# Graph layer on one core: output sums by DMA between DRAM tensors, earlier constants and loads, another general path

## The chip, the cores and the metric

One Trainium2 chip; the kernel runs on one of its cores, in one launch. The metric is the device time of an execution in microseconds (us). All times in this document are in us unless another unit stands beside them.

## The reference

x has N = 1250 nodes with D = 1024 features, in float32. There are E = 20000 edges (src, dst) with a type out of R = 8, and dst is sorted.

```python
h = jnp.maximum(_layernorm(x, axis=-1), 0.0)
# relational graph convolution on h, with edge_index = (src, dst)
u = h @ root + bias
for r in range(8):
    mask = edge_type == r
    sums = segment_sum(h[src] * mask[:, None], dst, N)
    cnt = segment_sum(mask, dst, N)
    u = u + (sums / maximum(cnt, 1)[:, None]) @ weight[r]
# highway
z = concatenate([u, h], axis=1) @ w_gate + b_gate
out = x + tanh(u) * z + h * (1 - z)
```

root and each weight[r] are 1024 x 1024, w_gate is 2048 x 1024.

## The kernel before, in words

**Order of the mathematics.** The kernel multiplies first and gathers afterwards: y = h @ weight[r] is computed for all nodes and stored to DRAM, and for each destination the rows y[src] of its edges are gathered and summed with their factors (1 / count). The output is made as (x + h) + the highway's rest: x + h is stored to `out` early, and at the end blocks of rows are scattered onto `out` by DMAs that add.

**Products.** Eleven matrices s are multiplied with the 1250 rows: s = 0 to 7 the relations, 8 the root, 9 (`LAST`) the lower half of w_gate, which meets h, and at the end the upper half, which meets u. The product is Strassen-Winograd's: seven smaller products, the *kinds* n = 0 to 6, of sums of quarters of h (left) with sums of quarters of the matrix (right), and each kind is again split in seven, with *inner sums* made beside it. s = 0 is done by blocks of rows (`product`, matmuls on L576), since the rows come in while it runs; s = 1 to 9 by kinds (`kind`). In a kind, in this order: two plain products into `xs`, then `left_sum(0)` x `right(0)` into the bank `ps_q`, `left_sum(1)` x `right(1)`, a plain one, DVE's additions on L427, `left_sum(2)` x `right(2)` into the bank that L427 has just read, and so on. TensorE's matmuls all have the lines L321 and L328.

**Inner sums.** `inner_sums(m, n, second)` makes them half by half. The right ones come from DVE (L276, L277 and L282, L283). The left ones are the same for every matrix: DVE makes them for s = 1 (L285, L286 and L279, L280), they are stored to `lefts_dram`, and for s > 1 a DMA on SP's queue loads each half (512 KB, L274), from the place in program order where the half's right sums are made. `loaded(s, n)` says for which kinds; with `LOADED = {}` for all but (9, 5) and (9, 6).

**What stands beside the products.** The program is written in one order, and each engine follows that order for its own instructions; SP's DMA queue too. The other work is spread over it by Python generators: within a kind, `call(k)`, k = 0 to 4, advances the generator by one `yield`. For the first two and a half matrices that generator is `norms_and_index` (L1346). Its parts:

- `norms()`: in s = 0 loads blocks of x, makes h = relu(layernorm(x)) in `Normed`, stores h to `h_dram`, and calls `with_x` (L1005): DVE adds x and h (L1009), SP stores the sum to `out` (L1010). The blocks are brought into the transposed layout `h_all` by DMA transposes (L540) with copies by ACT (L547) and DVE (L558).
- `columns()`: sorts out for every destination a table of its edges. Its last step is a DMA from POOL, table <- bits (L1213). Then the pool of buffers that it used is closed.
- `order()`: opens the pool "sort" in that room, and puts the nodes of each of three groups of relations in the order of their number of edges. `positions` (L864) begins with three iotas and a memset on POOL (L868 to L871), then compares on DVE (L872 to L874, L879, L885, ...) and makes ranks; `nodes_in_order` does one group's permutation with matmuls, and issues ten index gathers on POOL, idx <- table (L715). At the end `any_over` checks for destinations with too many edges.

The calls (4, k) for all k and (n, 3) for all n (`FULL_CALLS`, L78) are passed over. When `norms_and_index` has ended, the calls advance `beside_group`: for each of the three groups `counts(g)`, which counts edges by relation on DVE (memset L1384, pairs L758 and L759 over the index table).

At kind (3, 0) (L1690 to L1696) whatever is left of `beside_group` is flushed, and then `counts_over` (L1657) writes a branch that all engines pass: `If n_far > 0` (L1664) holds the general path for edges that fit no table (`far_ranks`, `order_again`, `counts`, `passes_over`). With this data it is not entered. From (3, 1) on the gathers begin: POOL's indirect DMA got <- y, idx (L1405), and DVE's multiply-add (L1410), for one slot of a block of 128 destinations.

**The end.** The last matrix is multiplied by blocks again, and `scatter_outs` adds finished blocks of rows to `out` (L726). The last block, of 98 rows, is scattered in pieces of columns, `PIECES`: one of 512 columns, then two of 256.

Of the kernel before, what the change touches and what calls it, by code (L numbers as in the profile page):

```python
# [9 lines left out]
F32 = mybir.dt.float32  # L10
BF16 = mybir.dt.bfloat16
# [10 lines left out]
def tile_rgcn_highway(  # L22
# [58 lines left out]
    LOADED = {}  # L81
# [45 lines left out]
    z_dram = dram.tile([N, D], F32, name="z_dram")  # L127
    codes_dram = dram.tile([WIN + NCH * P], I16, name="codes_dram")
# [134 lines left out]
    def inner_sums(m, n, second):  # L263


        b11, b12, b21, b22 = quarters(m.factor(n))
        a11, a12, a21, a22 = [left_of(n, o, k) for o in (0, 1) for k in (0, 2)]
        t1, t2, t3, t4 = [right(k) for k in range(4)]
        s1, s2, s3, s4 = [lefts[:, k].rearrange("p (u f) -> p u f", u=2) for k in range(4)]
        both = slice(2 * second, 2 * second + 2)  # L270
        kept = lefts_dram[n].rearrange("p (k n) -> p k n", k=KQ)[:, both]
        from_dram = loaded(m.s, n)
        if from_dram:
            nc.sync.dma_start(lefts[:, both], kept)  # L274
        if second:
            nc.vector.tensor_sub(t3, b22, b12)  # L276
            nc.vector.tensor_sub(t4, b21, t2)  # L277
            if not from_dram:
                nc.vector.tensor_sub(s3, a11, a21)  # L279
                nc.vector.tensor_sub(s4, a12, s2)  # L280
        else:
            nc.vector.tensor_sub(t1, b12, b11)  # L282
            nc.vector.tensor_sub(t2, b22, t1)  # L283
            if not from_dram:
                nc.vector.tensor_add(s1, a21, a22)  # L285
# [10 lines left out]
    def kind(m, n, between):  # L296
# [92 lines left out]
        if chained:  # L389
            rest()  # L390
            alone(range(KQ))
            alone_rows()
            call(0)
            m.make(n)
            for j, i in enumerate((0, 2, 1, 3)):
                add(banks[i], h_op[i][:, ORDER[n]], w, fresh=n not in (1, 5))
                if i == 2:
                    to_rows_of(0)
                if i == 0:
                    next_sums()  # L400
                call(j + 1)
            to_rows_of(1)
            return
# [22 lines left out]
        for u in range(2):  # L426
            nc.vector.tensor_add(banks[2 * u][:, H:], xs[u], ys[:, u * H:(u + 1) * H])  # L427
        call(1)
# [11 lines left out]
        for u in range(2):  # L440
            add(banks[2 * u][:, H:], left_sum(3)[:, u], b22)
        to_rows_of(0)
# [323 lines left out]
    def nodes_in_order(g, pos, ids_f, a, b, small, now=False, fresh=True):  # L766
# [5 lines left out]
        many = small[:, :P].bitcast(I16)[:, :P]  # L772
        hi_i, lo, hi, block = [small[:, P + k * ND:P + (k + 1) * ND] for k in range(4)]
        hi_i, lo, hi = hi_i.bitcast(I32), lo.bitcast(I16)[:, :ND], hi.bitcast(I16)[:, :ND]
        if fresh:
            nc.gpsimd.iota(many, pattern=[[1, P]], base=0, channel_multiplier=0)
            nc.vector.tensor_copy(block, many[:, :ND])
# [12 lines left out]
        while not now and at_call[2] != 2:  # L790
            yield
# [53 lines left out]
    def positions(runs, pos, ids_f, room, now=False):  # L845
# [17 lines left out]
        runs3 = runs.rearrange("p (g d) -> p g d", g=G)  # L863
        picked = room[1][:, :NHI * NCNT]  # L864
# [3 lines left out]
        nc.gpsimd.iota(many, pattern=[[1, P]], base=0, channel_multiplier=0)  # L868
        nc.gpsimd.iota(n_of, pattern=[[-1, NCNT]], base=SLOTS, channel_multiplier=0)
        nc.gpsimd.iota(step_of, pattern=[[1, ND], [-1, ND]], base=0, channel_multiplier=0)  # L870
        nc.gpsimd.memset(ones, 1.0)  # L871
# [26 lines left out]
        while not now and at_call[2] != 2:  # L898
            yield
# [23 lines left out]

    def passes_over():

        top = const.tile([1, 1], F32, name="top")
        largest((most[:, 0:1], top))
        whole(top, n_over, MORE - SLOTS, 0.0)
        nc.vector.tensor_single_scalar(n_over, n_over, 2, op=OP.arith_shift_right)
# [10 lines left out]
    with ExitStack() as early:  # L940
# [20 lines left out]
        class Normed:  # L961
# [43 lines left out]

            def with_x(self, to=None):
                n = self.n
                to = self.xt if to is None else to
                nc.vector.tensor_add(to[:n], self.xt[:n], self.ht[:n])  # L1009
                nc.sync.dma_start(out[self.d * P:self.d * P + n, :], to[:n])  # L1010
# [76 lines left out]
        runs = ix1.tile([P, NHI], F32, name="runs")  # L1087

# [127 lines left out]
        def order():  # L1216

            checks = [any_over]

            def rest_of_check():  # L1220
                if checks and at_call[0] and at_call[2] == 2:
                    checks.pop()()

            with tc.tile_pool(name="sort", bufs=1) as sp:
                pos = sp.tile([P, NHI], F32, name="pos")
                yield from positions(runs, pos, ids_f, [
                    sp.tile([P, n], F32, name=f"counted{k}")
                    for k, n in enumerate((D, *(NHI * NCNT // (1, 2, 2)[k] for k in range(3))))])
# [27 lines left out]
        def norms():  # L1256
# [12 lines left out]
            for b in b0:  # L1269
                b.with_x()  # L1270
# [4 lines left out]
            for b in b1:  # L1275
                b.with_x()
# [9 lines left out]
            b2[0].with_x(b2[0].ht)  # L1286
            b2[1].with_x()
# [19 lines left out]
            for b in b3:  # L1307
                b.with_x()
# [10 lines left out]
            for part in range(2):  # L1319
                ht = xpool.tile([P, D], F32, name="xt") if part else \  # L1320
                    h_op[4][:, S3:S4 + 1].rearrange("p a k f -> p (a k f)")
                if part:
                    b4[0].with_x()
# [10 lines left out]
            b4[1].with_x()  # L1334
# [10 lines left out]

        def norms_and_index():  # L1346

            later = index()
# [4 lines left out]
            for _ in later:  # L1353
                yield
# [18 lines left out]
    with ExitStack() as edges_part:  # L1373
# [264 lines left out]
        def order_again():  # L1638

            t = got()  # L1640
            runs, pos, ids_f = t[:, :NHI], t[:, NHI:2 * NHI], t[:, 2 * NHI:2 * NHI + ND]
            nc.vector.tensor_copy(ids_f, ids)
            in_table, is_edge = [
# [5 lines left out]
            room = [upool.tile([P, D], F32, name="u") for _ in range(4)]  # L1649
            for _ in positions(runs, pos, ids_f, room, True):  # L1650
                pass
            for g in range(G):
                for _ in nodes_in_order(g, pos[:, g * ND:(g + 1) * ND], ids_f,
                                        got().bitcast(BF16), got().bitcast(BF16), got(), True):
                    pass
# [115 lines left out]
        PIECES = ((2, Q), (4, H), (4, 0))  # L1771
# [96 lines left out]
        for i in range(NP):  # L1868
# [85 lines left out]
```

## Time and profile before

| | us |
|---|---|
| three timed runs | 1287.15, 1291.23, 1292.73 (median 1291.23) |
| the profiled execution, its own time | 1288.27 |
| its span, from first to last instruction | 1286.5 |
| PE busy | 1252.6 |
| DVE busy | 973.6 |
| POOL busy | 435.0 |
| ACT busy | 274.0 |

The granted clock of TensorE was 0.992 over the span. The DMA queues moved 315.90 MB, 246 GB/s on the mean.

PE is TensorE's matmuls, DVE the vector engine, ACT the scalar engine, POOL GpSimd; SPq is the queue of instructions of the sync engine, which here issues most DMAs. A row of a timeline gives the start, the duration, the engine, the line, the operation with what it writes and reads (buffer numbers left out), the shape and how many instructions are put together in the row; the bracket is the idle time of the engine just before, and what ended it ("issue": nothing that the profile shows). A row of a group gives the count, the busy sum and the mean in ns, then the idle time before. A row of the DMA issues gives the count and the KB of each or the median time from issue to landing. `out_dram<-h_all` or `<-xt` is the store of x + h, `counted` and `small` are buffers of the pool "sort", `bits` and `raw` of the pool before it.

### The profile page before, as it was taken

What the parts mean: (1) busy time and instruction counts of PE and PEld (TensorE: products, weight loads), DVE (VectorE), ACT (ScalarE), POOL (GpSimd) and SP (SyncE); (2) the same over time, 40 slices, a digit from 0 to 9 for tenths busy, and PEclk for the clock granted to TensorE, in tenths of its full rate; (3) what the DMA queues carried; (4) which work ended last, traced back from release to release, by engine and by line L of the source; (5) the groups of instructions that cost most, each with busy time, mean ns of one, the idle gap of its engine ahead of it and who ended that gap; (6) DMA issues with size and microseconds to landing.
All of it is one profiled execution on the core that took longest, in us unless ns stands there. A gap on an engine that the chain in (4) does not pass through costs nothing.

```text
span 1286.5 us, 14084 instructions
## 1 busy us (share of the span) xinstructions
PE 1252.6 (97%) x4725; PEld 885.3 (69%) x4725; DVE 973.6 (76%) x1459; ACT 274.0 (21%) x517; POOL 435.0 (34%) x393
## 2 busy tenths in 40 slices
PE   9999999899999999999999999999999999999996
PEld 5444777677767777777777777777777777544443
DVE  7665998676758787887887779898888797856642
ACT  3353211121112112112111211211221121202210
POOL 0430000017102222322432333463452467754532
PEclk9999999899999999999999999999999999999999
DMA  7786324834656686998898768899997969999983
GB/s 301 239 239 195 126 90 169 205 108 137 194 175 206 202 276 236 314 319 317 293 331 302 248 192 289 286 334 352 352 288 250 357 190 356 349 335 225 234 151 56
DMA packets 131088, 315.90 MB, mean 246 GB/s; under 512 B 30963, under 2 KB 32382, under 8 KB 131006
## 3 DMA queue, kind: packets, MB, share of 16 engines
q1 hardware_dynamic: 87678, 189.79, 42.6%
q0 software_dynamic: 43040, 124.60, 32.7%
q8 instruction: 38, 0.62, 0.2%
q10 hardware_dynamic: 288, 0.52, 0.1%
q14 instruction: 44, 0.36, 0.1%
HBM read 251.70 MB, written 85.06 MB: 262 GB/s over the span
## 4 chain that ended last, share of the span: by engine, by line
PE 45%; issue 9%; DMA 8%; POOL 6%; DVE 2%; ACT 0%; POOLq 0%; SPq 0%; DVEq 0%; ACTq 0%
PE ps_n L321 15%; PE ps L321 14%; PE ps_b L328 10%; DMA got<-y,idx 7%; PE ps_q L321 5%; POOL got L1405 2%; POOL out_dram L726 1%; PE ps_b L576 1%; POOL h_all L715 1%; DMA w<-lefts_dram 1%; POOL u L715 1%; PE ps_n L576 1%; DMA z_dram<-w 0%; DVE u L1410 0%; POOL w L715 0%
## 5 line engine op out<-in xcount | busy, mean ns | idle before, releaser
L1405 POOL DMA_INDIRECT got<-y,idx x205 | 253.3, 1236 | 446.8 <-DVE u L1410 338.7
L321 PE MATMUL ps<-w,h_all 128*128 128x256 f32 (+1 forms) x1040 | 258.7, 392 | 0.0
L1410 DVE SCALAR_TENSOR_TENSOR u<-got,w_of,u 128x1024 f32<-128x1024 f32 (+1 forms) x189 | 241.1, 1277 | 16.2 <-DMA got<-y,idx 15.8
L321 PE MATMUL ps_n<-w,w 128*128 128x256 f32 x976 | 236.3, 386 | 10.8 <-DVE ps L427 6.9
L321 PEld LDWEIGHTS ps_n<-w,w 128*128 128x128 f32 x976 | 187.3, 193 | 64.1 <-issue 23.8
L328 PE MATMUL ps_b<-w,h_all 128*128 128x512 f32 x504 | 226.6, 592 | 0.0
L321 PEld LDWEIGHTS ps<-w,h_all 128*128 128x128 f32 x1040 | 197.6, 190 | 39.7 <-issue 14.1
L328 PEld LDWEIGHTS ps_b<-w,h_all 128*128 128x128 f32 x504 | 95.8, 190 | 94.1 <-issue 90.9
L576 PE MATMUL ps_b<-w,h_all 128*128 128x512 f32 x312 | 140.0, 594 | 4.5 <-ACT h_all L547 1.6
L321 PE MATMUL ps_q<-w,w 128*128 128x256 f32 x488 | 116.1, 381 | 4.3 <-DMA w<-lefts_dram 2.2
L436 ACT COPY ps<-ps_n 128x512 f32<-128x512 f32 x122 | 64.6, 574 | 255.7 <-PE ps_n L321 255.7
L321 PE MATMUL ps<-w,w 128*128 128x256 f32 x488 | 116.3, 381 | 0.0
L321 PE MATMUL ps_n<-w,h_all 128*128 128x256 f32 x488 | 115.3, 379 | 0.4 <-PEq L1664 0.4
L576 PEld LDWEIGHTS ps_b<-w,h_all 128*128 128x128 f32 x312 | 58.3, 190 | 78.5 <-issue 68.6
L427 DVE TENSOR_TENSOR ps<-ps_n,inner 128x256 f32<-128x256 f32 x122 | 50.4, 429 | 75.7 <-PE ps L321 75.6
L321 PEld LDWEIGHTS ps_q<-w,w 128*128 128x128 f32 x488 | 92.6, 190 | 18.1 <-issue 2.5
L321 PEld LDWEIGHTS ps<-w,w 128*128 128x128 f32 x488 | 93.6, 192 | 13.0
L321 PEld LDWEIGHTS ps_n<-w,h_all 128*128 128x128 f32 x488 | 92.6, 190 | 13.8 <-PEq L1664 0.8
L413 ACT COPY ps<-ps_n 128x256 f32<-128x256 f32 x122 | 39.6, 360 | 245.6 <-PE ps_n L321 184.1
L236 DVE TENSOR_TENSOR w<-w,w 128x2048 f32<-128x2048 f32 x36 | 82.2, 2284 | 0.3
L576 PE MATMUL ps<-w,h_all 128*128 128x512 f32 (+1 forms) x136 | 57.7, 568 | 1.4 <-DVE h_all L558 1.4
L1213 POOL DMA_DIRECT2D table<-bits x1 | 1.7, 1707 | 145.5 <-DVE bits L1212 145.5
(250 smaller groups left out, 1181.4 us busy)
## 6 DMA issues: line engine op xcount, KB each, us to landing
w<-lefts_dram SPq DMA_DIRECT2D x108, 512.0 KB
w<-in_L_gnn_weight_dram SPq DMA_DIRECT2D x31, 1024.0 KB
y<-row SPq DMA_DIRECT2D x84, 256.0 KB
y<-w SPq DMA_DIRECT2D x42, 256.0 KB
w<-in_L_gnn_w_gate_dram SPq DMA_DIRECT2D x8, 1024.0 KB
lefts_dram<-w SPq DMA_DIRECT2D x14, 512.0 KB
h_dram<-h_all SPq DMA_DIRECT2D x9, 512.0 KB
y<-row SPq DMA_DIRECT2D x9, 512.0 KB
```

Source lines behind the costliest of these rows:

```text
L236: nc.vector.tensor_sub(w[to], w[a], w[b])
L321: nc.tensor.matmul(p, a[:, k], b[:, k], start=(fresh and k == 0), stop=(k == a.shape[1] - 1), skip_group_check=True)
L328: nc.tensor.matmul(to, h_op[NP - 1][:, ORDER[n], k], w[:, k], start=(fresh and k == 0), stop=(k == KQ - 1), skip_group_check=True)
L413: nc.scalar.copy(banks[2 * u][:, :H], xs[u])
L427: nc.vector.tensor_add(banks[2 * u][:, H:], xs[u], ys[:, u * H:(u + 1) * H])
L436: nc.scalar.copy(banks[2 * u + 1].rearrange("p (a n) -> p a n", a=2), xs[u][:, None, :].to_broadcast([P, 2, H]))
L576: nc.tensor.matmul(b[:, at], aop[:, i, k, :], w.of[i][:, k, at], start=(fresh and k == 0), stop=(k == KQ - 1), skip_group_check=True)
L715: nc.gpsimd.indirect_dma_start(out=to, out_offset=None, in_=of, in_offset=bass.IndirectOffsetOnAxis(ap=at, axis=0), compute_op=op)
L726: ins = nc.gpsimd.indirect_dma_start(out=of, out_offset=bass.IndirectOffsetOnAxis(ap=at, axis=0), in_=frm, in_offset=None, compute_op=op)
L1213: nc.gpsimd.dma_start(table.rearrange("(b p s) o -> p b (s o)", p=P, s=SLOTS), rows_in)
L1405: nc.gpsimd.indirect_dma_start(out=t[:n], out_offset=None, in_=y[g][:, :], in_offset=bass.IndirectOffsetOnAxis(ap=at[:n, d, k:k + 1], axis=0),
L1410: nc.vector.scalar_tensor_tensor(u[:n], t[:n], w, u[:n], op0=OP.mult, op1=OP.add)
```

## The change

1. **x + h.** `with_x` and its ten calls are removed. SP copies x to `out` from DRAM to DRAM, two blocks of 128 rows at a time, at call 1 of kinds n = 0, 1, 2, 3 and 5 of s = 1. In `order`, after each group's nodes, POOL issues DMAs that add h from `h_dram` onto `out`, also from DRAM to DRAM, 3, 3 and 4 of them. After the groups come two additional yields.
2. **Constants of `order`.** `positions` is started early: its iotas and the memset run at the start, into a buffer `counted0` of an older pool (`ix1`), as does `pos`. The first comparisons (L872 to L874) also use only that pool; L879 is the first to use "sort". `nodes_in_order` takes the iota `many` from there.
3. **Loads of left sums.** `load_sums` issues the load of a kind's first half before `call(1)` of the kind before, and of the second half after `left_sum(3)` of the kind before. `LOADED` leaves out (8, 5), (9, 1) and (9, 3): DVE makes these sums.
4. **General path.** `order_again` ranks nodes by comparing counts with a broadcast from DRAM, without TensorE, and `passes_over` transposes by DMA.
5. **Pieces.** The last block's scatter is two pieces of 512 columns.

```diff
-    LOADED = {}
+    LOADED = {8: (0, 1, 2, 3, 4, 6), 9: (0, 2, 4)}
...
-        if from_dram:
-            nc.sync.dma_start(lefts[:, both], kept)
...
+    def load_sums(s, n, second):
+
+        if n == 7:
+            s, n = s + 1, 0
+        if s <= LAST and loaded(s, n) and not regular(s, n):
+            both = slice(2 * second, 2 * second + 2)
+            nc.sync.dma_start(lefts[:, both],
+                              lefts_dram[n].rearrange("p (k n) -> p k n", k=KQ)[:, both])
...
             nc.vector.tensor_add(banks[2 * u][:, H:], xs[u], ys[:, u * H:(u + 1) * H])
+        load_sums(s, n + 1, 0)
         call(1)
...
             add(banks[2 * u][:, H:], left_sum(3)[:, u], b22)
+        load_sums(s, n + 1, 1)
         to_rows_of(0)
...
+        nc.gpsimd.iota(many, pattern=[[1, P]], base=0, channel_multiplier=0)
+        nc.gpsimd.iota(n_of, pattern=[[-1, NCNT]], base=SLOTS, channel_multiplier=0)
+        nc.gpsimd.iota(step_of, pattern=[[1, ND], [-1, ND]], base=0, channel_multiplier=0)
+        nc.gpsimd.memset(ones, 1.0)
+        yield many
         picked = room[1][:, :NHI * NCNT]
...
-            def with_x(self, to=None):
-                n = self.n
-                to = self.xt if to is None else to
-                nc.vector.tensor_add(to[:n], self.xt[:n], self.ht[:n])
-                nc.sync.dma_start(out[self.d * P:self.d * P + n, :], to[:n])
...
+        pos = ix1.tile([P, NHI], F32, name="pos")
+        counted = [ix1.tile([P, D], F32, name="counted0")]
+        placing = positions(runs, pos, ids_f, counted)
+        many = next(placing)
...
+                counted.extend([sp.tile([P, NHI * NCNT // n], F32, name=f"counted{k}")
+                                for k, n in ((1, 1), (2, 2), (3, 2))])
+                yield from placing
...
                 for g in range(G):
-                    yield from nodes_in_order(g, pos[:, g * ND:(g + 1) * ND], ids_f, junk, hot, room,
-                                              fresh=g == 0)
+                    yield from nodes_in_order(g, pos[:, g * ND:(g + 1) * ND], ids_f, junk, hot, room, many)
+                    assert not xh
+                    for d in range(g * ND // G, (g + 1) * ND // G):
+                        nc.gpsimd.dma_start(out[block(d)], h_dram[block(d)], accum_op=OP.add,
+                                            max_dma_last_dim=4 * D)
+                for _ in range(2):
+                    yield
                 while checks:
...
+            for d in range(ND):
+                xh.append((out[block(d)], x[block(d)]))
             later = index()
...
             for _ in later:
+                if xh and at_call[0] == 1 and at_call[2] == 1:
+                    for _ in range(2):
+                        nc.sync.dma_start(*xh.pop())
                 yield
...
+            for g in range(G):
+                for half in range(2):
+                    at = slice(half * KEYS // 2, (half + 1) * KEYS // 2)
+                    nc.gpsimd.dma_start(v_bc, val_dram[g:g + 1, at].to_broadcast([P, KEYS // 2]))
+                    for c in range(g * ND, (g + 1) * ND):
+                        to = pos[:, c:c + 1]
+                        nc.vector.scalar_tensor_tensor(junk, v_bc, val[:, c:c + 1],
+                                                       one.to_broadcast([P, KEYS // 2]),
+                                                       op0=OP.is_gt, op1=OP.mult,
+                                                       accum_out=part if half else to)
+                        if half:
+                            nc.vector.tensor_add(to, to, part)
...
-        PIECES = ((2, Q), (4, H), (4, 0))
+        PIECES = ((2, Q), (2, 0))
...
-                if more is not None:
+                if more is not None and c0 == 0:
                     scatter_piece(c0, t[1])
```

More of the change, by code (lines that the diff above doesn't have):

```diff
@@ L789, in nodes_in_order @@
         yield
-        while not now and at_call[2] != 2:
+        while at_call[2] != 2:
             yield
@@ L843, in to_table, with positions @@
         rests()
-    def positions(runs, pos, ids_f, room, now=False):
+    def positions(runs, pos, ids_f, room):
         used = [0]
@@ L897, in positions @@
         yield
-        while not now and at_call[2] != 2:
+        while at_call[2] != 2:
             yield
@@ L1268, in norms @@
             yield
-            for b in b0:
-                b.with_x()
             yield
@@ L1638, in order_again @@
         def order_again():
+            sizes = (NHI, NHI, NHI, NHI, ND, 1, 1)
             t = got()
-            runs, pos, ids_f = t[:, :NHI], t[:, NHI:2 * NHI], t[:, 2 * NHI:2 * NHI + ND]
+            runs, val, pos, pos_i, ids_f, one, part = [
+                t[:, sum(sizes[:k]):sum(sizes[:k + 1])] for k in range(len(sizes))]
+            pos_i = pos_i.bitcast(I32)
             nc.vector.tensor_copy(ids_f, ids)
+            nc.vector.memset(one, 1.0)
             in_table, is_edge = [
```

65 lines of the change are left out of this document (32 added, 33 removed).

## The prediction

> **What bounds the kernel now.** The page first: its span and its line of engines.
> ```profile
> span 1286.5 us, 14084 instructions
> PE 1252.6 (97%) x4725; PEld 885.3 (69%) x4725; DVE 973.6 (76%) x1459; ACT 274.0 (21%) x517; POOL 435.0 (34%) x393
> ```
> PE is busy for 97%. An edit that takes work from DVE, POOL or a queue therefore pays only where PE waits. The timeline of PE is read next, for gaps (the bracket is the idle time before the row's first matmul, and what ended it).
> ```profile
> 60.87 3.70 PE L576 MATMUL ps_b<-w,h_all 128*128 128x512 f32 x8 [0.93 <-ACT h_all L547]
> 65.93 3.70 PE L576 MATMUL ps<-w,h_all 128*128 128x512 f32 x8 [1.36 <-DVE h_all L558]
> 87.43 3.70 PE L576 MATMUL ps_b<-w,h_all 128*128 128x512 f32 x8 [0.63 <-ACT h_all L547]
> ...
> 247.53 3.78 PE L321 MATMUL ps_n<-w,w 128*128 128x256 f32 x8 [6.13 <-DVE ps L427]
> 251.10 2.87 PE L321 MATMUL ps<-w,w 128*128 128x256 f32 x8
> 257.26 1.89 PE L321 MATMUL ps_q<-w,w 128*128 128x256 f32 x8
> ...
> 367.18 1.97 PE L321 MATMUL ps_n<-w,h_all 128*128 128x256 f32 x8 [0.45 <-PEq L1664]
> 371.28 2.53 PE L321 MATMUL ps_q<-w,w 128*128 128x256 f32 x8 [2.13 <-issue]
> 373.61 3.05 PE L321 MATMUL ps_n<-w,w 128*128 128x256 f32 x8
> ...
> 918.42 1.97 PE L321 MATMUL ps_q<-w,w 128*128 128x256 f32 x8 [1.44 <-DMA w<-lefts_dram]
> 1028.70 1.97 PE L321 MATMUL ps_q<-w,w 128*128 128x256 f32 x8 [0.76 <-DMA w<-lefts_dram]
> 1096.06 3.68 PE L321 MATMUL ps_n<-w,w 128*128 128x256 f32 x8 [3.31 <-ACT ps L413]
> ```
> Eight undisturbed matmuls of this shape take 1.97. After a gap they are slower: 3.78 and 2.87 behind 6.13 idle, together 6.65 - 2 x 1.97 = 2.7 more; 3.68 behind 3.31 idle, 1.7 more. I call this the ramp and add it to a gap. Each part of the change aims at one of these gaps.
>
> **Part 1, x + h to the output.** In the first matrix SP stores x + h, made by DVE, and its queue is in order.
> ```profile
> 46.88 0.98 SPq L1010 DMA_DIRECT2D out_dram<-h_all  x2
> 48.86 7.57 SPq L540 DMA_TRANSPOSE inner<-h_all  x1
> ...
> 59.48 1.33 ACT L547 COPY h_all<-inner 128x1024 uint16<-128x1024 uint16 x1 [5.79 <-DMA inner<-h_all]
> ```
> The transpose is issued behind two 512 KB stores; the ACT copy waits 5.79 for it, and PE's gap at 60.87 waits for that copy. The two other gaps of the first matrix have the same chain behind them. Without the stores I take all three as gone: 0.93 + 1.36 + 0.63 = 2.9 (bounds: nothing, and 3.6 with slower matmuls behind them). The ten DRAM copies move to the second matrix, two at a time over five calls on SP.
> ```profile
> DMA  7786324834656686998898768899997969999983
> ```
> A digit is a slice of 32.2; that matrix lies in the slices from 129 to 257, with 3, 2, 4 and 8 tenths. There is room, so I cost the copies at nothing (at most 1, if a load behind them is late). The ten accumulating DMAs on POOL are a rival below.
>
> **Part 2, order's constants.** POOL's and DVE's timelines around 247:
> ```profile
> 233.05 1.71 POOL L1213 DMA_DIRECT2D table<-bits  x1 [145.49 <-DVE bits L1212]
> 245.97 0.23 POOL L868 IOTA counted<- 128x128 int16 x1 [11.22 <-DMA table<-bits]
> ```
> ```profile
> 247.38 0.90 DVE L879 TENSOR_TENSOR counted<-runs,counted 128x720 bf16<-128x720 f32 x1
> 252.16 0.68 DVE L282 TENSOR_TENSOR w<-w 128x512 f32<-128x512 f32 x1
> ```
> L868 writes into a pool that opens where another closes, whose last user, the table's DMA, lands at 245.97. DVE's comparisons wait for the iota, L427 is queued behind them, and PE for L427: 6.13 + 2.7 = 8.8. After the change iotas and first comparisons lie in an older pool: L427 no longer waits and PE starts at 247.53 - 6.13 = 241.4. But L879 is the first touch of the reopened pool, and I expect it to wait for the same DMA. It then begins at 245.97 instead of 247.38, 1.41 earlier, and L282, queued behind it, ends at 252.84 - 1.41 = 251.4. PE's work from 247.53 to ps_q takes 257.26 - 247.53 - 2.7 = 7.0, so PE comes to ps_q at 248.4 and waits 3.0 for L282; with 1.7 of ramp ps_q is as far along at 253.1 as before at 257.26: 4.1 gained. Bounds: 8.8 gained if L879 doesn't wait; 1 lost if the table lands later. I take 4.1, since L868 waited though its bytes need not be those that the DMA reads.
>
> The Trainium skill ("TensorE: Matmul & The Clock Gate", Part 1) has the array at half clock only after an idle window of about 3.4 us. By it the new gap of 3.0 has no ramp and the sum would be 1.7 lower. The trace disagrees: 2.53 and 3.05 stand behind an idle of 2.13.
>
> **Part 3, the general path and two more yields.** At 367 all engines pass the branch L1664 around the general path. PE's gaps 0.45 + 2.13 and the slower matmuls (2.53 + 3.05 - 3.94 = 1.6) are 4.2 in all; a body with under half of PE's instructions should take them away. But DVE passes too:
> ```profile
> 366.33 0.94 DVE L448 TENSOR_TENSOR ps<-ps,inner 128x256 f32<-128x256 f32 x2 [0.60 <-PE ps L321]
> 373.73 1.29 DVE L379 TENSOR_TENSOR w<-w,ps 128x512 f32<-128x512 f32 x2 [6.46 <-issue]
> ...
> 378.42 0.43 DVE L427 TENSOR_TENSOR ps<-ps_n,inner 128x256 f32<-128x256 f32 x1 [0.36 <-PE ps L321]
> ```
> ```profile
> 381.82 1.73 PE ps_n L321 x8
> ```
> DVE loses 6.46 here. The two yields put the check of order two calls later, so that the generator of the counts has one call left before the branch, where the rest is flushed: counts(1) and counts(2).
> ```profile
> L1384 DVE MEMSET got<- 128x1024 f32 x3 | 2.7, 912 | 0.5 <-issue 0.5
> L758 DVE TENSOR_SCALAR got<-idx 128x220 f32<-128x220 int32 x8 | 2.2, 270 | 0.8 <-issue 0.5 <-DMA idx<-table,node_key 0.3
> L759 DVE TENSOR_REDUCE got<-got 128x10 f32<-128x220 f32 x8 | 3.1, 384 | 0.3
> ```
> Two groups are two memsets and five pairs: 2 x 0.91 + 5 x (0.27 + 0.38) = 5.1, with their share of the idle and small sums about 6.1. DVE ends L448 at 367.27; with 6.1 and 6.46 L379 starts at 379.8. From L379 to the end of the second L427 DVE has 4.1 of work (378.85 - 373.73, less waits of about 1): 383.9. The matmuls that need it began at 381.82: 2.1 late. PE, no longer stalled itself, would be there at 381.82 - 4.2 = 377.6, idles over 6 us and pays a ramp of 2.7: 4.8 lost. Bounds: 3.9 gained (no flush in the way: DVE at 377.9), 4.8 lost. I take the loss.
>
> **Part 4, left sums.** SP's timeline, the loads behind the gaps at 918 and 1028:
> ```profile
> 904.94 0.32 SPq L274 DMA_DIRECT2D w<-lefts_dram  x1
> ...
> 1018.09 0.38 SPq L274 DMA_DIRECT2D w<-lefts_dram  x1
> ```
> SP runs ahead of the engines and issues a load when the buffer is free, unless a store stands before it. The first was issued 13.5 before its use; an earlier place can't help, the transfer itself was slow: nothing. The second came late behind stores: 0.8 gained. Three kinds, (8,5), (9,1), (9,3), are no longer loaded; 6 of 108 loads go and DVE makes those sums with four additions each, of about 0.68:
> ```profile
> L285 DVE TENSOR_TENSOR w<-h_all 128x512 f32<-128x512 f32 x7 | 4.8, 684 | 0.0
> ```
> ```profile
> 1083.95 1.89 PE L321 MATMUL ps_n<-w,w 128*128 128x256 f32 x8
> ```
> ```profile
> 1053.11 0.69 DVE L337 TENSOR_TENSOR row<-row,ps_b 128x512 f32<-128x512 f32 x1 [1.50 <-PE ps_b L328]
> ...
> 1082.03 0.76 DVE L427 TENSOR_TENSOR ps<-ps_n,inner 128x256 f32<-128x256 f32 x2
> 1088.58 1.28 DVE L1410 SCALAR_TENSOR_TENSOR u<-got,w_of,u 128x1024 f32<-128x1024 f32 x1 [4.61 <-DMA got<-y,idx]
> ```
> That is 2.7 per kind. The sums of (9,1) and (9,3), 5.5, fall between 1038 and 1083, where DVE's only idle time of note is the 1.50 above. L427 ends at 1082.79, PE begins the matmuls behind it at 1083.95: 1.2 of slack. 5.5 - 1.5 - 1.2 = 2.8 could show on PE, 4.6 with a ramp of 1.8. Against it the gap at 1096 (3.31 + 1.7) lies behind 4.61 that DVE waited for a gather, in DMA queues that now carry 3 MB less. I take zero (bounds -5.0 and +4.6).
>
> **Part 5, the tail.** The last two scatters, of 256 columns each, become one.
> ```profile
> 1277.04 0.42 DVE L1881 SCALAR_TENSOR_TENSOR row<-row,h_all 98x256 f32<-98x256 f32 x1
> ...
> 1278.56 1.52 POOL L726 DMA_INDIRECT out_dram<-row,piece_at  x1 [0.20 <-issue]
> ```
> The data are there at 1277.46, the last scatter started at 1278.56 behind the other piece's; it can start some 0.9 earlier. For twice the bytes I take 0.3 back: 0.6 gained (bounds 0.9 and nothing).
>
> **Sum.** -2.9 - 4.1 + 4.8 - 0.8 + 0 - 0.6 = -3.6. The profiled execution took 1288.27, so 1284.7 by its own time. The runs shown are 1291.23, 1287.15 and 1292.73; the mean of all four is 1289.85, and 3.6 below it is 1286.2.
>
> **Rivals.**
> (a) L879 finds its pool free: part 2 gains 8.8, 4.7 more: 1281.5. For it: its tiles need not overlap what the DMA reads. Against: nor had L868's.
> (b) The counts' flush isn't late: part 3 gains 3.9 instead of losing 4.8: 1277.5. For it: it takes only two generator calls more than I counted before the branch, or work between that DVE can still do while PE is ahead. Against: by my count the flush stands behind L448 in program order, and DVE and PE both pass the branch directly after it.
> (c) Slower: the accumulating DMAs hold back the indices. POOL's queue is one, and six of 512 KB come before group 2's index gathers.
> ```profile
> 298.43 0.95 POOL L715 DMA_INDIRECT idx<-table,node_key  x1 [0.30 <-issue]
> h_all<-h_dram,node POOLq DMA_INDIRECT x6, 9.7
> ```
> The nearest row, a 512 KB gather, lands in 9.7; six in a row end at 298 + 58 = 356, before the flush at 367. The point that decides is (367 - 298)/6 = 11.5 each. At 15 each the indices land at 388, DVE waits some 18 more at the branch, with PE behind it: 1304. No row of before shows a transfer from DRAM to DRAM that adds. The Trainium skill ("DMA: Bandwidth & Descriptors", the anatomy of one DMA on the SWDGE path) has 2.0 us plus bytes at 436 GB/s; an estimate by it is 3.2 each, and the sum would stay as it is.
> (d) DVE is the bound in the last kinds: part 4 costs 4.6: 1290.8.
>
> **How the numbers follow.** Forecast 0.46, (a) 0.15, (b) 0.16, (c) 0.09, (d) 0.14. The forecast's own range is 1281 to 1292 (the bounds of parts 1, 4 and 5, and 2 us of spread between runs). The range reaches below (b) where (a) joins it, and above (d) to part way into (c): 1273 to 1299. A measurement tells about 0.5%, 6.5 us, from no change: faster is below 1284.8, slower above 1297.7. Faster: (a), (b) and a third of the forecast, 0.45; slower: (c) and a little of (d), 0.12; the rest 0.43.
>
> **What would show it.** Part 1: no gaps over 0.5 on PE at 60, 66 and 87, and ACT's copies without 5.79 of waiting. Part 2: the 6.13 gone, and L879 behind the table's DMA with a gap of 3 before ps_q; (a) has no gap there. Part 3: no "issue" gap on PE at the branch, and a gap of some 6 before left_sum(2) that ends with L427; L758 rows right before the branch. If they stand earlier, (b). Part 4: the gap at 1028 gone, that at 918 there, and at 1084 no new gap; (d) shows one. (c) shows index gathers landing after 367. The forecast is wrong above all if part 2 or 3 turns over, each worth more than the rest together.

## The result, and the profile after

The changed kernel takes 0.9957 of the time before, 95% interval 0.9944 to 0.997: median 1287.82 of 22 runs (1283.34 to 1292.16) beside 1292.97 of 22 (1287.15 to 1299.74). 0.43% of 1292.97 is 5.6 less; 3.6 had been forecast, and both lie within the 0.5% called no change. The sum held. Most of its terms did not: they were off in both directions and cancelled, which was luck.

The page of the changed kernel, its span and its engines:
```profile
span 1281.5 us, 14045 instructions
PE 1249.9 (98%) x4725; PEld 883.1 (69%) x4725; DVE 970.8 (76%) x1462; ACT 274.4 (21%) x517; POOL 443.7 (35%) x400
```
PE still bounds it. The rows of PE's timeline that answer to those of before (lines have moved: L321 is L330 here, L427 is L438, L274 is L296, L448 is L461, L379 is L388, L758 in the counts is L771):
```profile
249.11 3.27 PE L330 MATMUL ps_q<-w,w 128*128 128x256 f32 x8 [4.48 <-DMA w<-lefts_dram]
...
346.39 1.97 PE L330 MATMUL ps_q<-w,w 128*128 128x256 f32 x8 [0.38 <-DMA w<-lefts_dram]
...
375.50 3.43 PE L330 MATMUL ps_n<-w,w 128*128 128x256 f32 x8 [4.74 <-DVE ps L438]
...
1000.01 1.99 PE L330 MATMUL ps_n<-w,w 128*128 128x256 f32 x8 [1.16 <-DVE ps L438]
...
1007.75 1.97 PE L330 MATMUL ps_q<-w,w 128*128 128x256 f32 x8 [0.56 <-DMA w<-lefts_dram]
...
1081.00 1.99 PE L330 MATMUL ps_n<-w,w 128*128 128x256 f32 x8 [1.11 <-DVE ps L438]
...
1090.48 1.99 PE L330 MATMUL ps_n<-w,w 128*128 128x256 f32 x8 [0.57 <-ACT ps L424]
```
The three gaps of the first matrix are gone, and so are those at 918 and 1028. The gap at 247 moved to ps_q and ends with a load, no longer with DVE's additions. The gap at the branch is longer than before and ends with DVE.

To compare kernels stage by stage, the next table gives PE's lost time: the start-to-start distances of successive matmuls less their undisturbed value (0.2155 for 256 columns, 0.4295 for 512, the trace's medians to within 0.001), summed over the same matmuls in every kernel. It holds idle time and ramps together. A ramp shows in the windows as a lower granted clock (the number before the DMA share and GB/s): 0.66 from 375 to 380 in the changed kernel, behind the gap of 4.74, and 1.00 around the same matmuls in no_yields (experiment 1), which has no gap there:
```profile
375.00:380.00 5.00, 4.50 (x13) 3.65 (x14) 4.83 (x8) 1.00 (x2) 1.10 (x1) 0.66 0.33 105
```
```profile
370.00:380.00 10.00, 10.00 (x40) 7.33 (x39) 9.69 (x16) 3.62 (x7) 2.05 (x2) 1.00 0.56 178
```
Stage limits are times of the kernel before; the stretches left out differ by 1.6 at most. The last row is the sum over all matmuls.

| lost on PE, us | before | changed | loads at the old place | x + h by DMA alone | general path alone | early loads alone | no late yields | early_dve |
|---|---|---|---|---|---|---|---|---|
| first matrix, 0 to 130 | 7.9 | 4.2 | 4.3 | 6.8 | 8.1 | 10.3 | 5.8 | 4.1 |
| order starts, 225 to 262 | 9.2 | 6.4 | 7.9 | 8.4 | 8.1 | 9.4 | 7.0 | 0.0 |
| branch, 340 to 390 | 4.8 | 7.4 | 8.4 | 7.1 | 0.5 | 2.1 | 0.8 | 0.3 |
| 850 to 960 | 1.8 | 0.1 | 7.5 | 0.6 | 2.7 | 0.1 | 0.4 | 0.5 |
| last kinds, 960 to 1200 | 9.4 | 10.6 | 12.0 | 10.1 | 10.5 | 9.1 | 12.6 | 11.2 |
| all | 37.9 | 33.0 | 44.3 | 38.4 | 34.7 | 36.8 | 31.6 | 21.0 |

One execution stands behind each column, and not a typical one in each: that of the changed kernel is the fastest of its 22 (1283.34), those of the general path alone and of early_dve are the fastest of theirs, that of no_yields is the slowest of its six. The first matrix and the last kinds differ by up to 2.4 between columns that have the same code there; a stage difference is relied on below only where a row names its cause.

### The profile page after: what moved, and what is told of

The parts are those of the page before. It is cut to its first block, busy times and chain, and to the rows that moved or that the text cites. A ratio compares the mean times of both kernels' runs of the same rounds, so it can differ in the third digit from the quotient of the medians.

```text
span 1281.5 us, 14045 instructions
## 1 busy us (share of the span) xinstructions
PE 1249.9 (98%) x4725; PEld 883.1 (69%) x4725; DVE 970.8 (76%) x1462; ACT 274.4 (21%) x517; POOL 443.7 (35%) x400
## 4 chain that ended last, share of the span: by engine, by line
PE 43%; issue 10%; DMA 7%; POOL 7%; DVE 2%; POOLq 0%; ACT 0%; DVEq 0%; SPq 0%; ACTq 0%
PE ps_n L330 14%; PE ps L330 14%; PE ps_b L337 9%; DMA got<-y,idx 5%; PE ps_q L330 4%; POOL got L1407 3%; DMA z_dram<-w 2%; PE ps_b L589 1%; POOL h_all L728 1%; POOL out_dram L739 1%; POOL u L728 1%; PE ps_n L589 1%; POOL w L728 0%; DVE h_all L1412 0%; DVE u L1412 0%
## 5 line engine op out<-in xcount | busy, mean ns | idle before, releaser
L1407 POOL DMA_INDIRECT got<-y,idx x205 | 256.0, 1249 | 435.5 <-DVE u L1412 332.6
L330 PE MATMUL ps<-w,h_all 128*128 128x256 f32 (+1 forms) x1040 | 258.7, 392 | 0.0
L330 PE MATMUL ps_n<-w,w 128*128 128x256 f32 x976 | 234.2, 383 | 9.2 <-DVE ps L438 7.3
L330 PEld LDWEIGHTS ps_n<-w,w 128*128 128x128 f32 x976 | 185.0, 191 | 63.2 <-issue 22.2
L330 PEld LDWEIGHTS ps<-w,h_all 128*128 128x128 f32 x1040 | 197.4, 190 | 39.6 <-issue 14.1
L330 PE MATMUL ps_q<-w,w 128*128 128x256 f32 x488 | 116.8, 383 | 5.4 <-DMA w<-lefts_dram 5.4
L448 ACT COPY ps<-ps_n 128x512 f32<-128x512 f32 x122 | 64.8, 575 | 252.5 <-PE ps_n L330 209.1
L330 PE MATMUL ps<-w,w 128*128 128x256 f32 x488 | 115.6, 380 | 0.0
L330 PE MATMUL ps_n<-w,h_all 128*128 128x256 f32 x488 | 115.3, 379 | 0.0
L438 DVE TENSOR_TENSOR ps<-ps_n,inner 128x256 f32<-128x256 f32 x122 | 50.5, 430 | 75.0 <-PE ps L330 67.8
L330 PEld LDWEIGHTS ps_q<-w,w 128*128 128x128 f32 x488 | 93.1, 191 | 19.4 <-DVE w L388 4.8
L330 PEld LDWEIGHTS ps<-w,w 128*128 128x128 f32 x488 | 93.1, 191 | 12.8
L330 PEld LDWEIGHTS ps_n<-w,h_all 128*128 128x128 f32 x488 | 92.7, 190 | 13.0 <-issue 0.5
L728 POOL DMA_INDIRECT idx<-table,node_key x30 | 32.5, 1082 | 58.6 <-DVE small L788 47.9
```

The costliest lines, as they stand in the source:

```text
L330: nc.tensor.matmul(p, a[:, k], b[:, k], start=(fresh and k == 0), stop=(k == a.shape[1] - 1), skip_group_check=True)
L448: nc.scalar.copy(banks[2 * u + 1].rearrange("p (a n) -> p a n", a=2), xs[u][:, None, :].to_broadcast([P, 2, H]))
L728: nc.gpsimd.indirect_dma_start(out=to, out_offset=None, in_=of, in_offset=bass.IndirectOffsetOnAxis(ap=at, axis=0), compute_op=op)
L1407: nc.gpsimd.indirect_dma_start(out=t[:n], out_offset=None, in_=y[g][:, :], in_offset=bass.IndirectOffsetOnAxis(ap=at[:n, d, k:k + 1], axis=0),
```

## The experiments

Each ratio is to the kernel before, timed on the same chip. Three groups were run, on chips where the kernel before had medians of 1288.97, 1290.07 and 1294.45; ratios of one group are compared first. Comparisons with the 0.9957 of the changed kernel cross groups, and each carries the widths of two intervals. The labels part1_alone and part4_alone count the items of the change: item 4 is the general path, which is Part 3 of the prediction, and the loads are its Part 4.

**1. The two late yields (no_yields).** The changed kernel without them:

```diff
-                for _ in range(2):
-                    yield
                 while checks:
```

> The changed kernel without the two yields after the groups. Theory: the gap of 4.74 and its ramp of 1.6 at 375 in the changed kernel come from the counts' flush of 7 that stands on DVE right before the branch; without the yields the counts lie earlier between the kinds and the gap is gone, 6.4 less than the changed kernel, about 0.991 of the kernel before. Rival: the gap is DVE's own 3.5 at the branch, flush or not: it stays at about 5, and the time stays at 0.996.

Measured: 0.9922 (0.9899 to 0.9944), median 1279.3. In the changed kernel DVE's timeline at the branch reads:
```profile
361.17 0.91 DVE L1386 MEMSET got<- 128x1024 f32 x1 [0.20 <-issue]
...
367.80 0.18 DVE L774 TENSOR_TENSOR rcp<-got 128x20 f32<-128x20 f32 x1
371.50 1.29 DVE L388 TENSOR_TENSOR w<-w,ps 128x512 f32<-128x512 f32 x2 [3.52 <-DVEq L1702]
...
374.71 0.73 DVE L438 TENSOR_TENSOR ps<-ps_n,inner 128x256 f32<-128x256 f32 x2
```
and without the yields, DVE first and then PE:
```profile
363.49 0.43 DVE L461 TENSOR_TENSOR ps<-ps,inner 128x256 f32<-128x256 f32 x1 [0.43 <-PE ps L330]
368.10 1.29 DVE L388 TENSOR_TENSOR w<-w,ps 128x512 f32<-128x512 f32 x2 [4.18 <-DVEq L1700]
```
```profile
370.12 3.60 PE L337 MATMUL ps_b<-w,h_all 128*128 128x512 f32 x8
373.56 1.89 PE L330 MATMUL ps_n<-w,w 128*128 128x256 f32 x8
```
The flush, 361.17 to 367.98, is 6.8 long and is what made DVE late: without it DVE still waits 4.18 at the branch, yet PE passes with no gap. The stage falls from 7.4 to 0.8. The theory holds; by the ratios 4.5 of these 6.6 show in the time, with some 3 of uncertainty from the two intervals.

**2. What holds ps_q at 249 (yields_early).** The two yields moved ahead of L890:

```diff
         yield
+        yield
+        yield
         of_n = n_of[:, None, :].to_broadcast([P, NHI, NCNT])
...
-                for _ in range(2):
-                    yield
                 while checks:
```

> The two yields stand before L890, the first instruction that waits for the table's DMA, instead of after the groups, so that L282, L283 and L388 of kind (2,0) are ahead of that wait on DVE. Both theories: the gap at the branch is gone (6.4). Theory, load: ps_q of (2,0) waits for the load of its left sums, which lands at 249 behind the table's DMA; its gap of 4.5 stays whether DVE is free or not: 0.991 of before. Rival, L890 (the prediction's): L282 behind L890 holds ps_q; the gap goes, 6.3 more: 0.986.

Measured: 0.9919 (0.9897 to 0.9941). First DVE of the changed kernel, then DVE and PE of this one:
```profile
242.12 0.91 DVE L890 TENSOR_TENSOR counted<-runs,counted 128x720 bf16<-128x720 f32 x1 [7.36 <-DMA table<-bits]
...
246.88 0.69 DVE L282 TENSOR_TENSOR w<-w 128x512 f32<-128x512 f32 x1
```
```profile
235.90 0.68 DVE L282 TENSOR_TENSOR w<-w 128x512 f32<-128x512 f32 x1
```
```profile
250.51 3.75 PE L330 MATMUL ps_q<-w,w 128*128 128x256 f32 x8 [4.66 <-DMA w<-lefts_dram]
```
L282 is ready 11 earlier, and the gap at ps_q is the same. The time is that of no_yields (0.9922), where the rival had 0.986. The right sums were not what came last; the load was. The rival falls.

**3. No load there (early_dve).** As 2, and DVE makes the left sums of kind (2,0):

```diff
-    LOADED = {8: (0, 1, 2, 3, 4, 6), 9: (0, 2, 4)}
+    LOADED = {2: (1, 2, 3, 4, 5, 6), 8: (0, 1, 2, 3, 4, 6), 9: (0, 2, 4)}
```

> As yields_early, and the left sums of kind (2,0) are made by DVE (four additions, 2.7) and not loaded. Theory, load: now nothing of (2,0) waits for a transfer behind the table's, the gap of 4.5 at ps_q and its ramp are gone: 0.986 of before. Rival, L890: 0.986 as well, but then yields_early has it already and this kernel is no faster than that one.

Measured: 0.9881 (0.9859 to 0.9904), median 1274.03. DVE and PE:
```profile
235.83 0.68 DVE L285 TENSOR_TENSOR w<-h_all 128x512 f32<-128x512 f32 x1
...
241.85 0.91 DVE L891 TENSOR_TENSOR counted<-runs,counted 128x720 bf16<-128x720 f32 x1
```
```profile
242.57 1.89 PE L330 MATMUL ps_n<-w,h_all 128*128 128x256 f32 x8
244.30 1.89 PE L330 MATMUL ps_q<-w,w 128*128 128x256 f32 x8
```
The gap and its ramp are gone (stage 0.0). Two of the four sums lie in the time in which DVE had waited for the table, the other two (from 246.56) hold up no matmul. The runs are 1271.45 to 1276.37, those of yields_early in the same group 1277.4 to 1279.81. The theory holds: PE waited for the load. What made the load late is not separated by it. The load was issued into the table's DMA, but in SP's queue a store of left sums, two stores of y and 1024 KB of weights also stand just ahead of it.

**4. The new general path alone (part4_alone).** The kernel before with `order_again` and `passes_over` of the change, nothing else.

> The kernel before with the new general path alone. Theory: engines stall at the branch by the length of the code that is jumped over; PE's 0.45 and 2.13 and the slow matmuls behind them go (4.2), and DVE's 6.46 falls to about 3.5 as in the changed kernel: 0.9967 of before. Rival: the stall is a fixed price of a branch, PE's stays: 1.000.

Measured: 0.9995 (0.9979 to 1.0012). PE and DVE at the branch:
```profile
365.72 1.89 PE L323 MATMUL ps_n<-w,h_all 128*128 128x256 f32 x8
367.45 1.89 PE L323 MATMUL ps_q<-w,w 128*128 128x256 f32 x8
```
```profile
371.88 1.28 DVE L381 TENSOR_TENSOR w<-w,ps 128x512 f32<-128x512 f32 x2 [5.45 <-DVEq L1695]
```
PE's 0.45 and 2.13 and the ramp are gone, as the theory says: 4.3 in the stage, and 3.2 in the span of the profiled execution (1283.3). The timed runs do not show it: 4.2 lies outside their interval, and the profiled execution is the fastest of the twelve (1285.08, median 1289.45). The theory on DVE's wait falls too: 5.45 here with the new path, 4.35 in part1_alone with the old one, so the body's length alone does not set it.

**5. x + h by DMA alone (part1_alone).** The kernel before with part 1, without the two yields.

> The kernel before with part 1 alone: x copied to the output, h added by DMA, no additional yields. Theory: the three gaps of the first matrix (0.93, 1.36, 0.63) come from transposes behind the stores and go; the copies and the ten accumulating DMAs lie beside other work: 2.9 less, 0.9977 of before. Rival 1: the gap at 66 waits for DVE's L571 and is there without the stores too; 1.5 less, 0.999. Rival 2: the accumulating DMAs hold back index gathers or loads and the gain is lost: 1.000 or more, and L715 or L758 show waits at 300 to 370.

Measured: 1.0011 (0.9995 to 1.0027). PE's gaps at 61 and 66 are gone, one at 86 stays, and at 353 there is a new one:
```profile
86.39 3.70 PE L576 MATMUL ps_b<-w,h_all 128*128 128x512 f32 x8 [0.96 <-ACT h_all L547]
...
353.03 1.97 PE L321 MATMUL ps_q<-w,w 128*128 128x256 f32 x8 [1.84 <-DMA w<-lefts_dram]
```
POOL's timeline and the windows (us, then busy time of PE, PEld, DVE, ACT and POOL with instructions, granted clock, DMA share, GB/s) show why:
```profile
330.68 3.59 POOL L1231 DMA_DIRECT2D out_dram<-h_dram  x4
```
```profile
340.00:350.00 10.00, 10.00 (x40) 7.29 (x40) 6.85 (x17) 1.06 (x2) 0.00 (x0) 1.00 1.05 304
```
In the kernel before the same window reads:
```profile
340.00:350.00 10.00, 10.00 (x41) 7.29 (x40) 7.09 (x17) 1.06 (x2) 0.00 (x0) 1.00 0.60 212
```
The last four accumulating DMAs go out at 331, and DMA is full from 340 to 350, with a share of 1.05 instead of 0.60; from 340 to 346 POOL's queue alone holds 79.8% of the DMA engines. A load of left sums is late; loads_old_place below, which has part 1 and late loads too, has the same gap at 349. What it wins in the first matrix (1.1 in the table) it pays there: rival 2 in its effect, but on the loads. Index gathers are not late: the counts of this kernel wait 0.3 for them, as in the kernel before, and those of the changed kernel wait for none:
```profile
L771 DVE TENSOR_SCALAR got<-idx 128x220 f32<-128x220 int32 x8 | 2.2, 274 | 0.9 <-issue 0.8
```

**6. Loads at the old place (loads_old_place).** The changed kernel with

```diff
         from_dram = loaded(m.s, n)
+        if from_dram:
+            nc.sync.dma_start(lefts[:, both], kept)
```

and the calls of `load_sums` gone.

> The changed kernel with each load at its old place in the program, LOADED as changed. Theory (the prediction's): an earlier place gives SP nothing where it already ran ahead; the gap at 918 is there or not as the transfers fall, a gap like that of 0.76 at 1028 comes back: at most 1 more, 0.9957 to 0.9965 of before. Rival: the place matters, the gaps of 1.44 and 0.76 both come back, and also that at 249 in kind (2,0) grows since its load is issued later: 4 or more, 0.999.

Measured: 1.0043 (1.0028 to 1.0058): slower than the kernel before, and 0.9% slower than the changed one. SP's queue here, and then that of the changed kernel, at the same kind:
```profile
900.92 0.32 SPq L482 DMA_DIRECT2D y<-row  x1
901.52 0.70 SPq L482 DMA_DIRECT2D y<-w  x1
903.49 0.32 SPq L276 DMA_DIRECT2D w<-lefts_dram  x1
```
```profile
900.61 0.32 SPq L296 DMA_DIRECT2D w<-lefts_dram  x1
901.02 0.38 SPq L484 DMA_DIRECT2D y<-row  x1
901.50 5.22 SPq L484 DMA_DIRECT2D y<-w  x2
```
PE's use of that load, here and in the changed kernel, and the windows here:
```profile
920.78 3.52 PE L332 MATMUL ps_q<-w,w 128*128 128x256 f32 x8 [5.25 <-DMA w<-lefts_dram]
```
```profile
912.48 1.89 PE L330 MATMUL ps_q<-w,w 128*128 128x256 f32 x8
```
```profile
910.00:915.00 5.00, 5.00 (x25) 4.41 (x24) 3.46 (x7) 1.06 (x2) 3.25 (x4) 1.00 1.04 415
915.00:920.00 5.00, 0.53 (x3) 0.13 (x1) 2.92 (x4) 0.63 (x2) 0.99 (x1) 1.00 1.03 414
```
In both the load is issued when its buffer is free, 12.0 and 11.9 before PE is ready for it (920.78 - 5.25 - 903.49 and 912.48 - 900.61), but at the old place two stores of y stand ahead of it that otherwise come behind. DMA moves 414 GB/s with a share over 1.0. The load was used 17.3 after issue, in the changed kernel 11.9 after, without a wait. The rival holds, and the prediction's view falls. That the stores ahead are the whole cause is not shown: their 512 KB are 1.3 at 414 GB/s. POOL's queue, which carries the gathers, held 52.7% of the DMA engines between issue and use; SP's queue moved 3.44 MB in these 17.3, some 200 KB per us, and at that rate the two stores are 2.6 of the 5.25.

**7. All left sums loaded (loaded_all).** The changed kernel with `LOADED = {}`.

> The changed kernel with LOADED = {}, so all left sums are loaded again, but from the early place. Theory: the last kinds were limited by transfers, and making three kinds' sums on DVE is what took the gap of 3.31 at 1096; it comes back (3 to 5 with its ramp), and the gaps of 1.1 that end with DVE's L438 at 1000 and 1081 go: 2.5 more than the changed kernel, about 0.998 of before. Rival: the early place of the loads did it; without DVE's 8 of additions the last kinds are as fast or faster: 0.994 to 0.996.

Measured: 0.9978 (0.9964 to 0.9993), 0.65% below loads_old_place of the same group. In the last kinds:
```profile
1005.23 1.99 PE L330 MATMUL ps_n<-w,w 128*128 128x256 f32 x8 [2.12 <-DVE ps L438]
...
1094.58 2.78 PE L330 MATMUL ps_n<-w,w 128*128 128x256 f32 x8 [2.85 <-ACT ps L424]
```
The gap of 3.31 at 1096 comes back with the loads and that at 1081 goes, as the theory says, but a gap at DVE's L438 stays and the sum over the last kinds is 10.3, beside 10.6 for the changed kernel. The two intervals overlap, and they come from different groups: not told apart. The early place does not always spare PE the load at 918: here PE still waits 1.19 for it, at 916.66.

**8. The early place alone (loads_early_alone).** The kernel before with `load_sums` at its three places and `LOADED = {}`.

> The kernel before with only the early place of the loads (LOADED = {}). The changed kernel with loads at the old place was 1.0043 of before, with them early 0.9957. Theory, queue order: a load issued ahead of the y stores lands ahead of them, wherever DMA is full; the gaps at 918 and 1028 go, and more in executions where transfers fall worse: 0.991 to 0.995. Rival, only together: the early place only repairs what the copies and accumulating DMAs of part 1 add to the queues; alone it is worth the two gaps of before, 2.2, or 0.998.

Measured: 0.9935 (0.992 to 0.995). Theory: held. The rows of the group of ps_q, in the kernel before, in loads_old_place and here (count, busy, mean ns, then the idle time before them and what ended it):
```profile
L321 PE MATMUL ps_q<-w,w 128*128 128x256 f32 x488 | 116.1, 381 | 4.3 <-DMA w<-lefts_dram 2.2 <-issue 2.1
```
```profile
L332 PE MATMUL ps_q<-w,w 128*128 128x256 f32 x488 | 119.0, 388 | 12.8 <-DMA w<-lefts_dram 7.5 <-DVE w L390 5.2
```
```profile
L328 PE MATMUL ps_q<-w,w 128*128 128x256 f32 x488 | 115.4, 379 | 1.1 <-issue 1.1
```
In this execution no matmul waits for a load any more. 0.65% is 8.4 of 1294.45, more than the whole change gained, and more than the 2.2 that the one profiled execution of before has to win. part4_alone and part1_alone, also with late loads, have 4.7 each in this row: how much waits for loads differs between executions. That it makes up the rest of the 8.4 is argued, not shown: the two profiled executions differ by 1.1 in their span (1286.5 and 1285.4), since the first matrix loses 2.4 more here, and the other timed executions have no trace.

**9. Early loads and the new general path (loads_early_part4).** 8 and 4 together.

> As loads_early_alone, with the new general path too. Part 4 alone took 4.3 of waiting from PE at the branch and yet gave 0.9995. Theory: the gain was lost again in loads that landed no earlier (gaps 2.5 and 2.5 at 914 and 1010 there); with the loads early it stays: 3 to 4 less than loads_early_alone. Rival: what comes behind (gathers on DVE and POOL in the last kinds) takes it back: the same as loads_early_alone within 1.5.

Measured: 0.9933 (0.9911 to 0.9954), median 1283.27 of ten runs, where 8 had 0.9935 and 1286.65 of six. By the ratio the general path adds nothing, by the medians 3.4. PE's loss in the branch stage is 0.2 (2.1 in 8). Whether the time keeps what PE no longer waits stays open.

**10. Part 1 undone in the better kernel (early_dve_with_x).** early_dve with x + h by DVE and SP's stores.

> early_dve with part 1 undone: x + h made by DVE and stored by SP in the first matrix again, no DMA that adds. Theory: with the loads early, nothing waits for the accumulating DMAs any more, and part 1 is worth its gaps in the first matrix, 2.5: this kernel is at 0.990, early_dve at 0.988. Rival: part 1 is worth nothing or less, since its 15 MB of traffic come back elsewhere (part1_alone was 1.001): 0.988 or below.

Measured: 0.9864 (0.9846 to 0.9882). Not slower than early_dve (0.9881, 0.9859 to 0.9904, in another group): no gain from x + h by DMA can be seen in the time, though the first matrix loses 9.2 on PE here and 4.1 there.

**11. The late kinds loaded again (early_dve_loaded).** early_dve with `LOADED = {2: (1, 2, 3, 4, 5, 6)}`.

> early_dve with the left sums of (8,5), (9,1) and (9,3) loaded again (only (2,0) is made by DVE). Theory: what these sums cost on DVE in the last kinds and what their loads cost in the queues is about the same: 0.988 within 0.15%. Rival 1, transfers limit the last kinds: 2.5 slower, 0.990. Rival 2, DVE limits them: 2.5 faster, 0.986.

Measured: 0.9854 (0.9836 to 0.9871), median 1276.07, 0.1% from 10 in the same group. Beside early_dve's 0.9881, of another group, the loads of (8,5), (9,1) and (9,3) cost no more than the additions; rival 1 falls, rival 2 (0.986) can't be told from the theory by these intervals.

**12. Three pieces (pieces_old).** The changed kernel with the old `PIECES`.

> The changed kernel with the last block scattered in three pieces again. Theory: one scatter of 512 columns saves 0.6 behind the last matmul: the stretch from PE's end to the end of the span is 0.6 longer here than the changed kernel's 9.8. Rival: what starts earlier lands no earlier, since the bytes are the same: the stretch is the same within 0.2.

One execution: behind PE's last matmul 10.3 remain, 9.8 in the changed kernel, 9.9 in the kernel before. Over the other profiled kernels this stretch is 9.9 to 10.2 with three pieces and 9.4 to 10.2 with two: 0.6 is within what it varies by. Inconclusive.

**The better versions.** 3, 10 and 11 are 1.2 to 1.5% faster than the kernel before and, by the quotients of these ratios with 0.9957, 0.8 to 1.0% faster than the changed one, with the same remedy: the counts spread out before the branch, and nothing of kind (2,0) loaded behind the table's DMA.

## Why the prediction was right, and where its steps were wrong

**The bound** was right: every gain and loss that a trace above explains is a wait of PE.

**Part 1, 2.9 gained: mis-sized.** The stores did delay a transpose: the ACT copy that had waited 5.79 for it stands at 53.66 in the changed kernel, without a wait. The next copy still waits 5.80 for its own transpose, and in four other kernels without the stores (no_yields, yields_early, loaded_all, pieces_old) PE waits 1.4 to 1.9 at 64 or 65 for DVE's L571, which in no_yields waits for that copy. So the stores were not the only cause of the gaps. Over all profiled kernels the first matrix loses 4.1 to 6.8 without the stores and 7.9 to 10.3 with them. But "there is room, so I cost the copies at nothing" looked only at the copies of x and not at the ten DMAs that add; those were weighed as a danger to index gathers. They delayed the loads of left sums instead (1.84 at 353), and the part alone is worth 1.4 lost, with an interval from 0.6 gained to 3.5 lost: a gain of 2.9 is excluded, a loss is not shown.

**Part 2, 4.1 gained: mechanism right, size off, 2.7.** L890 waited for the table (7.36), as forecast, and rival (a) is out. L282 ended 2.9 after PE was ready (247.57 against 242.74 + 1.89 = 244.63); forecast 3.0. The step that failed is taking L282 as the last to come: the load, issued behind the table's DMA, came 1.5 later, and experiment 2 shows that it would have held PE alone. The gap became 4.48 and its ramp 3.27 + 2.31 - 3.94 = 1.6, together 6.1 in place of 8.8. Part 2 was not timed alone.

**Part 3, 4.8 lost: mechanism right, size off, 2.6 in the trace.** The flush stands where it was forecast (6.8; forecast 6.1), PE's own stall is gone, PE waits 4.74 for L438. DVE's wait at the branch was 3.52 instead of 6.46, so the stage loses 2.6 more than before, not 4.8. The yields cost 4.5 by the ratios (experiment 1). Rival (b) is out, since the flush does stand right before the branch. What the new path itself gives, 4.3 in a trace, is not seen in the time.

**Part 4, 0.8 gained: the step that was wrong.** "The first was issued 13.5 before its use; an earlier place can't help, the transfer itself was slow." Measured from when PE is ready for it, the time of issue did not change (12.0 before, 11.9 after), but the order in SP's queue did, and the wait of 5.25 at the old place was none at the new one (experiment 6). The early place is worth 8.4 alone (experiment 8, 6.5 to 10.4 by its interval), ten times the term. The sums made by DVE were put at zero: the two gaps traded as described (1096 shrank, 1081 appeared, 1.11 instead of up to 2.8, so rival (d) is partly there), and the net can't be told from zero.

**Part 5, 0.6 gained: not measurable.**

**Rival (c)** did not happen. Its price for one transfer was right: in part1_alone nine of these DMAs take a median of 9.6 from issue to landing, beside the 9.7 of the gather. Wrong was to set six of them end to end. POOL's timeline in the changed kernel:
```profile
293.07 2.71 POOL L1237 DMA_DIRECT2D out_dram<-h_dram  x3
...
306.12 0.94 POOL L728 DMA_INDIRECT idx<-table,node_key  x1 [0.66 <-DMA out_dram<-h_dram]
```
The three are issued within 2.71, and a gather that waits for one of them goes on at 306.1, 13.0 after the first was issued; end to end they would have taken 29. The gathers lose 2.5 by it in all, and the last is issued at 326.65, long before the branch. The estimate by the Trainium skill ("DMA: Bandwidth & Descriptors", the SWDGE path), 3.2 for one, is a third of the measured 9.6; that the sum would stay as it is was right all the same.

**The sum.** With what was measured in place of the terms: +1.4 - 2.7 + 4.5 - 8.4 and about zero for the rest is 5.2 gained, beside 5.6 measured; it mixes ratios and one trace, and each of the ratios has an interval of some 2 us or more to either side, so the agreement is luck as well. It says only that errors of opposite sign, 4 too good on part 1 and 8 too little on the loads, hid behind a forecast that came true.

## What to carry to other kernels

Where DMA is full, a load's time depends also on what stands ahead of it in its queue; put the load ahead of the stores that nobody waits for, and look at the order of issue, not only at its time. When one wait is removed, list everything that the next instruction needs, transfers included, and ask which comes last. A total that agrees is no proof of its terms; each one wants its own run.

## What the runs showed that was not expected

The place of 512 KB loads among the stores of one queue, with DMA full at 414 GB/s, is worth 0.65% of this kernel (experiment 8; 0.9% by experiment 6), without a change in any engine's work.

The table's DMA has little to move (330 KB) but lands only at 242.12, and ahead of that the DMA engines are full while little moves. The windows of the changed kernel:
```profile
235.00:240.00 5.00, 5.00 (x19) 3.28 (x18) 0.00 (x0) 1.06 (x2) 0.00 (x0) 1.00 0.98 67
```
A share of 0.98 at 67 GB/s, and the load issued into it at 236.96 reached PE only at 249.1. Which transfer holds the engines the row doesn't tell. The kernel before has the same stretch (0.96 at 83 GB/s from 240 to 245).

PE's stall at the branch (2.13, 2.38 and 1.1 in three kernels with the old general path) is absent in all profiled kernels with the new one, while DVE's wait there is 4.35, 5.45 and 6.46 with the old and lies between 3.52 and 5.45 with the new.
